# Transfers that build the sums of x, issued step by step, and output stores on another queue

## Chip, cores and metric

The kernel runs on one core of a Trainium2 chip. The metric is the time of one execution on the device in microseconds (us), as the median of several runs; less is better. The core has five engines with a queue of instructions each: TensorE (PE in the profile; its weight loads are PEld), VectorE (DVE), ScalarE (ACT), GpSimd (POOL) and SyncE (SP). An engine takes its queue in order and waits at an instruction until the data it needs is there. SP and POOL are used here to issue transfers (DMAs), which 16 DMA engines carry out. SP's transfers form one DMA queue, POOL's another.

## The reference

Four images x of 128 channels and 96 x 96 pixels go through two non-local blocks, one after the other. A block is attention over pixels: every one of the 9216 pixels is a query, and the 2304 pixels of a 2 x 2 max-pooled map are the keys and values.

```python
g_x     = maxpool2(conv1x1(x, g_w, g_b))        # values, 64 channels x 2304
theta_x = conv1x1(x, theta_w, theta_b)          # queries, 64 channels x 9216
phi_x   = maxpool2(conv1x1(x, phi_w, phi_b))    # keys, 64 channels x 2304
f    = jnp.einsum('bqc,bck->bqk', theta_x, phi_x)
attn = jax.nn.softmax(f, axis=-1)
y    = jnp.einsum('bqk,bkc->bqc', attn, g_x)
W_y  = conv1x1(y, W_w, W_b)                     # back to 128 channels
W_y  = W_y * inv + (bn_beta - bn_mean * inv)    # batch norm, inference form
return W_y + x
```

The output of the first block is the input of the second. Everything is float32.

## The kernel before

**Blocks, pairs, slots.** Four images times two layers make eight blocks, in the order of `ORDER`. An image stays in one SBUF tile `xt` [128, 9216], and a block adds its result into that tile. A block has nine *pairs* of 1024 queries. The keys are 18 tiles of 128, and a pair works through them in nine *slots* of two tiles: TensorE makes the scores of two tiles (L584), ScalarE their exponentials (L589), VectorE adds these up (L596, L598), and TensorE multiplies the exponentials of the slot before with the values (L606). There are 72 pairs, so 648 slots. Two pairs, an "even" and an "odd" one, make a *cycle* of 18 slots (`CYCLE`), numbered 0 to 17. One loop over `t` (L904) writes all slots out; whatever else is to be done hangs on a slot number of it. For TensorE, VectorE, ScalarE and SP this written order is the order of their queues (`manual_schedule`, L98 to L100). POOL isn't in that list: the framework's scheduler orders POOL's queue.

**The end of a pair.** When all values of a pair are summed, ScalarE copies the result out of PSUM into a tile `halves` (L613, `values`). There are two such tiles, so a pair takes the tile of the pair two before it. This copy is at slot 9 for the even pair and at slot 0 of the next cycle for the odd one. `turn` and `invert` make 1 / (sum of exponentials) on VectorE (L656 to L674). `invert` stands at slot 13 for the even pair and at slot 6 of the next cycle for the odd one. It ends with eight transfers on SP's queue: four that write the inverses as rows into a corner of the tile `stage` (L680) and four that spread each row over 64 partitions of `halves` (L685). `normalise` (L695) multiplies by them, at slots 1 and 10 of the next cycle. `multiply` (L701) projects back to 128 channels at slots 3 and 13 of the next cycle, and `add` follows at once: ScalarE adds the shift (L712), and POOL issues a transfer that adds `halves` into `xt` (L716, "the x add"). In the second layer POOL then issues the store of these pixels to the output (L726). The last two pairs do without the adding transfer.

**Units: keys and values of the next block.** While a block runs, the keys and values of the next one are made in six *units* of 16 image rows, two units in 18 slots. A unit makes its products with fewer multiplications, by use of sums of parts of x: `sums[0]` ("one"), `sums[1]` ("two"), each with a low half (partitions 0 to 63) and a high half, and `half`, a copy of half of `two[high]` in the low partitions. These tiles exist once and are used by all units in turn. A unit has four stages on TensorE, at the slots of `UNITS`: 15, 16, 18, 20 for units 0, 2, 4 of a block and 25, 26, 28, 30 for units 1, 3, 5, counted from the start of the cycle and 18 more for each further two units. The first stage reads x alone. The second reads `two[high]` (L460) and then, at the end of its slot and ahead of the values, `half` (`second_rest`, L463, seen as L441 `unit_ps<-stage`, since `half` lies in `stage`). The third reads `one`, the fourth `two[low]`.

**Building the sums.** `build` and `build_rest` (L412 to L430) issue the transfers. SP loads `one` (L416) and `two[high]` (L417) out of `xt`. POOL adds into `one[high]` and `one[low]` (L422, twice, `sums<-x`) and adds `one[high]` into `two[high]` (L422, `sums<-sums`, "the high add"). SP then copies `half` (L423), loads `two[low]` (L429), and POOL adds `two[high]` into it (L430). For unit 0 all this is written at slot 9 of the block's first cycle (`BUILD`). For the others `build` is written at the slot of the third stage of the unit before it, and `build_rest` at that of the fourth.

Of the kernel before, what the change touches and what calls it, by code (L numbers as in the profile page):

```python
# [12 lines left out]
ALU = mybir.AluOpType  # L13
# [3 lines left out]
P = 128  # L17
B, C, CI, H, W = 4, 128, 64, 96, 96
# [14 lines left out]
PT = 2 * QT  # L33
# [6 lines left out]
UN = 4 * W  # L40
# [1 line left out]
UB = 2 * UK // 32  # L42
TB = NKT // 2
UNITS = ((15, 16, 18, 20), (25, 26, 28, 30))
BUILD = 9
AFTER = ((1, 1, 2, 4, 5), (1, 2, 2, 3, 4))
THETAS = (6, 5)

# [6 lines left out]
CYCLE = 2 * NB  # L55
# [6 lines left out]
def shifted_blocks(ctx: ExitStack, tc: tile.TileContext, x: bass.AP, layers, out: bass.AP, flag):  # L62
# [24 lines left out]
    nc = tc.nc  # L87
# [26 lines left out]
    sums = [const.tile([P, 2, UN], F32, name=f"sums_{i}") for i in range(2)]  # L114
# [4 lines left out]
    def load_x(b, n=6):  # L119
        xt = xp.tile([C, HW], F32, tag="x", name=f"x_{b}")  # L120
        src = x[b].rearrange("c h w -> c (h w)")
        for i in range(n):
            nc.sync.dma_start(out=xt[:, ts(i, HW // n)], in_=src[:, ts(i, HW // n)])
        return xt
# [274 lines left out]
    class Unit:  # L399
# [12 lines left out]
        def build(self):  # L412

            low, high = slice(0, CI), slice(CI, P)
            one, two = sums
            nc.sync.dma_start(out=one, in_=self.pixels(0, slice(0, P)))  # L416
            nc.sync.dma_start(out=two[high], in_=self.pixels(1, low))  # L417
            for dst, src in (
                (one[high], self.pixels(0, low)), (two[high], one[high]),
                (one[low], self.pixels(1, low)),  # L420
            ):
                nc.gpsimd.dma_start(out=dst, in_=src, accum_op=ALU.add)  # L422
            nc.sync.dma_start(out=self.half, in_=two[high, :, UN // 2 :])  # L423

        def build_rest(self):

            low, high = slice(0, CI), slice(CI, P)
            two = sums[1]
            nc.sync.dma_start(out=two[low], in_=self.pixels(1, high))  # L429
            nc.gpsimd.dma_start(out=two[low], in_=two[high], accum_op=ALU.add)  # L430

        def both(self, *some):
            for c in range(2):
# [25 lines left out]
        def second(self):  # L459
            self.part(self.blk.w.mixed[CI:, 0, :], sums[1][CI:, :, : UN // 2], 0)  # L460
# [80 lines left out]
    class Pair:  # L541
# [164 lines left out]
        def add(self):  # L706

            cols = ts(self.p, PT)
            here = self.blk.xt[:, cols]
            if self.number < late:  # L710
                for h in range(2):
                    nc.scalar.activation(  # L712
                        self.halves[:, ts(h, QT)], self.pss[h], AF.Identity,
                        bias=self.blk.w.shift,
                    )
                nc.gpsimd.dma_start(out=here, in_=self.halves, accum_op=ALU.add)  # L716
                engine = nc.gpsimd
            else:
                for h in range(2):
                    dst = here[:, ts(h, QT)]  # L720
                    nc.vector.scalar_tensor_tensor(
                        dst, self.pss[h], self.blk.w.shift, dst, op0=ALU.add, op1=ALU.add
                    )
                engine = nc.sync
            if self.blk.store is not None:
                engine.dma_start(out=self.blk.store[:, cols], in_=here)  # L726

        def finish(self, check, result):

# [34 lines left out]
    def thetas(both):  # L764
        pss = two_banks(f"theta_ps_{both[0].name}")

        def part(i, rows, c):
            pair = both[i]
            return (
                pss[i][ts(c, CI), :], pair.blk.w.theta[rows, :],  # L770
                pair.blk.xt[rows, ts(2 * pair.p + c, QT)],
            )

        def take():
            for i in range(2):
                both[i].take_theta(pss[i])

        return crosswise(part, take)
# [20 lines left out]
    def begin(n):  # L799

        blocks[n].xt = xs[ORDER[n][0]]
        blocks[n].begin_keys()
# [66 lines left out]
    def later(t, step):  # L869
        tails.setdefault(t, []).append(step)  # L870

    for n in range(1, len(blocks)):
        cycle = (n - 1) * NP * NB // CYCLE * CYCLE
        for u in range(NU):
            unit = Unit(blocks[n], u)
            at = [cycle + u // 2 * 2 * CYCLE // 2 + i for i in UNITS[u % 2]]
            for i, t in enumerate(at):
                assert t not in stages
                stages[t] = (unit, i)
            if u == 0:  # L880
                later(cycle + BUILD, lambda n=n: begin(n))
                later(cycle + BUILD, unit.build)
                later(cycle + BUILD, unit.build_rest)
            else:
                later(free[0], unit.build)
                later(free[1], unit.build_rest)
            free = at[2:]
            when = [at[3] + i for i in AFTER[u % 2]]
            later(when[0], lambda unit=unit: unit.pool(1))
            if u == 0:  # L890
                later(when[0], unit.centring)
            later(when[1], lambda unit=unit: unit.pool(0))
            later(when[2], unit.spread)
            for i in range(2):
                later(when[3 + i], lambda unit=unit, i=i: unit.square(i))
# [8 lines left out]
    for t in range(total + 1):  # L904
        q, s = 2 * (t // CYCLE), t % CYCLE
        even, odd = pairs[q : q + 2] if t < total else (None, None)
        first, second, take = None, *pending
        pending = (None, None)
        unit, stage_of = stages.get(t, (None, None))
        assert unit is None or (t not in keys and second is None)  # L910
        if t in keys:
            n, i = keys[t]
            first, *pending = blocks[n].chunks(i)
        elif unit:
            first = (unit.first, unit.second, unit.third, unit.fourth)[stage_of]
            second = unit.second_rest if stage_of == 1 else None
            take = (unit.first_sum, unit.second_sum, unit.third_sum, unit.fourth_sum)[stage_of]
        elif t < total and s == THETAS[q > 0]:
            if q < late:
                first, *pending = thetas(pairs[q + 1 : q + 3])  # L920
            else:
                first, take = odd.theta_alone()
        elif t == total - 1:
            second, take = even.multiply, even.add
        elif gone and s in PROJECT:
            pair = gone[PROJECT.index(s)]
            second, take = pair.multiply, pair.add
        if t < total:
            now, j = divmod(t, NB)
            if s == 0 and q:  # L930
                gone = pairs[q - 2 : q]
            if t in loads:
                xs[loads[t]] = load_x(loads[t])
        for i in range(KB):
            if t < total:
                pairs[now].scores(j * KB + i, rowwise=stage_of == 1 and i == 1)
            if i == 0 and first:
                first()
        if second:
            second()  # L940
        for i in range(KB):
            if t < total:
                pairs[now].add_up(j * KB + i)
            if i == (stage_of == 1) and take:
                take()
        if t == 0:
            b0.batch(FIRST - 1)
        if t - 1 in keys and t < NB:
            b0.batch(keys[t - 1][1])
        if t:  # L950
            before, j = divmod(t - 1, NB)
            for k in ends.get(t, range(j * KB, (j + 1) * KB)):
                pairs[before].values(k)
        if t < total:
            for i, pair in enumerate(gone):
                if s == NORM[i]:
                    pair.normalise()
            for i, pair in enumerate((even, gone[1] if gone else None)):
                if pair is None:
                    continue  # L960
                if s in (TURNS[i], TURNS[i] + 1):
                    pair.turn(s - TURNS[i])
                sooner = q == late and i == 0
                if s == (TURNS[0] + 2 if sooner else HALVES[i]):
                    pair.add_halves()
                if s == (TURNS[0] + 2 if sooner else INVERT[i]):
                    pair.invert()
            if q == late and s == 15:
                even.normalise()
        if t == total - 1:  # L970
            odd.last_denominators()
        for i, k in squares.get(t, []):
            b0.square(i, k)
        for step in tails.pop(t, []):
            step()
        for step in after.pop(t, []):
            step()
# [323 lines left out]
```

## Time and profile before

| | us |
|---|---|
| median of 3 runs | 2540.0 |
| lowest, highest | 2537.94, 2541.27 |
| the profiled execution, its own time | 2539.5 |
| its span, first to last instruction | 2537.7 |

The mean granted clock of TensorE in the profiled execution is 0.995 of full speed. Some groups of instructions and transfers that the change touches or that stand near it:

| line | engine | what | times | mean or median |
|---|---|---|---|---|
| L613 | ACT | copy of `halves` out of PSUM | 71 | 1012 ns |
| L716 | POOL | issue of the x add, 512 KB | 70 | 5.3 us to landing |
| L726 | POOL | issue of a store, 512 KB | 34 | 3.2 us to landing |
| L422 | POOL | adds from x, 192 KB | 84 | 4.7 us to landing |
| L422, L430 | POOL | adds from a sum, 192 KB | 84 | 4.0 us to landing |
| L416 | SP | load of `one`, 384 KB | 42 | |
| L417, L429 | SP | loads of `two`, 192 KB | 84 | |
| L423 | SP | copy of `half`, 96 KB | 42 | |
| L680 | SP | rows of inverses, 1 KB | 284 | |
| L685 | SP | rows spread over 64 partitions, 64 KB | 284 | |

How to read what is shown further on. In the list of waits a line says which engine and line waited for which, then the total in us, the number of times and the longest. A timeline line gives the start in us from the span's start, the length in us, the engine (with q: its queue's own work, such as the issue of a transfer), line, operation, the tiles written and read, shapes and number, and in brackets the idle time before it with what ended it. For a transfer the length is that of its issue, not of its movement; when it has landed shows in whoever waits for it. A table by stretches gives the stretch, its length, then the busy time and number of instructions of each engine, the granted clock, the busy share of the DMA engines and GB/s.

### The profile page before, as it was taken

What the parts mean: (1) busy time and instruction counts of PE and PEld (TensorE: products, weight loads), DVE (VectorE), ACT (ScalarE), POOL (GpSimd) and SP (SyncE); (2) the same over time, 40 slices, a digit from 0 to 9 for tenths busy, and PEclk for the clock granted to TensorE, in tenths of its full rate; (3) what the DMA queues carried; (4) which work ended last, traced back from release to release, by engine and by line L of the source; (5) the groups of instructions that cost most, each with busy time, mean ns of one, the idle gap of its engine ahead of it and who ended that gap; (6) DMA issues with size and microseconds to landing.
All of it is one profiled execution on the core that took longest, in us unless ns stands there. A gap on an engine that the chain in (4) does not pass through costs nothing.

```text
span 2537.7 us, 56492 instructions
## 1 busy us (share of the span) xinstructions
PE 2487.6 (98%) x23391; PEld 945.2 (37%) x23391; DVE 2190.6 (86%) x2947; ACT 1671.8 (66%) x1836; POOL 233.9 (9%) x278
## 2 busy tenths in 40 slices
PE   9998999999999999998999999999999999999998
PEld 5344453433333333333333333333333333333333
DVE  7997988998879997997887999799987899878777
ACT  5665666666666666665666666666666666666664
POOL 0011001100011101110001110111000111000000
PEclk9999999999999999999999999999999999999999
DMA  5356444553356535555335663555434555333333
GB/s 181 42 78 131 41 51 65 73 62 26 26 84 87 85 45 82 75 69 125 26 26 83 87 87 43 82 75 72 55 23 38 77 86 94 43 43 42 40 38 52
DMA packets 96981, 167.62 MB, mean 66 GB/s; under 512 B 17346, under 2 KB 74060, under 8 KB 96716
## 3 DMA queue, kind: packets, MB, share of 16 engines
q1 hardware_dynamic: 62756, 76.29, 26.9%
q0 software_dynamic: 33792, 87.57, 20.3%
q8 instruction: 185, 3.03, 0.5%
q14 instruction: 80, 0.66, 0.1%
q10 hardware_dynamic: 168, 0.07, 0.0%
HBM read 19.21 MB, written 18.87 MB: 15 GB/s over the span
## 4 chain that ended last, share of the span: by engine, by line
PE 73%; DMA 16%; DVE 6%; issue 2%; ACT 2%; SPq 2%; POOL 0%; DVEq 0%; POOLq 0%; ACTq 0%
PE av L606 33%; PE sc L584 33%; DMA x<-halves 8%; DMA sums<-x 4%; DVE sum L598 3%; PE unit_ps L435 2%; PE theta_ps L268 2%; PE W_ps L701 2%; DMA sums<-sums 1%; ACT exp L589 1%; DMA halves<-stage 1%; SPq L680 1%; SPq L685 1%; ACT halves L613 1%; DMA stage<-both 0%
## 5 line engine op out<-in xcount | busy, mean ns | idle before, releaser
L589 ACT ACTIVATE exp<-sc,nshift 128x1024 f32<-128x1024 f32 x1296 | 1396.6, 1114 | 720.2 <-PE sc L584 708.0
L598 DVE TENSOR_TENSOR sum<-sum,exp 128x1024 f32<-128x1024 f32 x1151 | 1407.5, 1223 | 244.1 <-ACT exp L589 184.6
L584 PE MATMUL sc<-theta,phi 64*64 64x512 f32 x10368 | 1291.8, 590 | 3.1 <-ACT exp L589 3.0
L606 PE MATMUL av<-exp,gT 64*64 64x512 f32 x10368 | 1249.8, 592 | 29.4 <-ACT halves L613 29.3
L606 PEld LDWEIGHTS av<-exp,gT 64*64 64x64 f32 x10368 | 418.1, 133 | 715.1 <-issue 651.6
L584 PEld LDWEIGHTS sc<-theta,phi 64*64 64x64 f32 x10368 | 424.2, 133 | 680.0 <-issue 589.5
L422 POOL DMA_DIRECT2D sums<-x x84 | 82.4, 1160 | 836.9 <-DMA sums<-x 535.2
L716 POOL DMA_DIRECT2D x<-halves x70 | 70.8, 1011 | 836.9 <-ACT halves L712 836.8
L613 ACT COPY halves<-av 128x1024 f32<-128x1024 f32 x71 | 71.9, 1012 | 75.1 <-DMA x<-halves 49.8
L596 DVE TENSOR_TENSOR sum<-exp,exp 128x1024 f32<-128x1024 f32 x72 | 88.0, 1222 | 30.3 <-ACT exp L589 30.2
L657 DVE TENSOR_REDUCE parts<-turned 128x16 f32<-128x512 f32 x142 | 97.4, 686 | 4.9
L656 DVE STREAM_TRANSPOSE turned<-sum 128x512 f32<-128x512 f32 x142 | 100.1, 705 | 0.5
L712 ACT ACTIVATE halves<-W_ps,shift 128x512 f32<-128x512 f32 x140 | 88.8, 694 | 0.8 <-PE W_ps L701 0.8
L701 PE MATMUL W_ps<-halves,WT 64*64 64x512 f32 x568 | 75.2, 590 | 3.8 <-DVE halves L695 3.6
L495 DVE TENSOR_REDUCE stage<-stage 128x192 f32<-128x768 f32 x84 | 77.8, 940 | 0.0
L536 DVE STREAM_TRANSPOSE gT<-stage 32x192 f32<-32x192 f32 (+1 forms) x224 | 71.5, 319 | 3.8
L268 PE MATMUL theta_ps<-x,thetaT 64*64 64x512 f32 x560 | 74.0, 589 | 0.0
L695 DVE TENSOR_TENSOR halves<-halves 128x512 f32<-128x512 f32 x71 | 48.7, 685 | 26.7 <-DMA halves<-stage 26.7
L435 PE MATMUL unit_ps<-sums,mixed 64*64 64x384 f32 x504 | 70.2, 484 | 0.0
L430 POOL DMA_DIRECT2D sums<-sums x42 | 33.8, 805 | 303.9 <-DMA stage<-both 131.4
L669 DVE STREAM_TRANSPOSE four<-parts 32x32 f32<-32x32 f32 x284 | 56.4, 198 | 2.9
L692 DVE TENSOR_TENSOR halves<-halves 128x512 f32<-128x512 f32 x71 | 48.5, 683 | 0.0
(114 smaller groups left out, 753.9 us busy)
## 6 DMA issues: line engine op xcount, KB each, us to landing
x<-halves POOLq DMA_DIRECT2D x70, 512.0 KB, 5.3
halves<-stage SPq DMA_DIRECT2D x284, 64.0 KB
out_dram<-x POOLq DMA_DIRECT2D x34, 512.0 KB, 3.2
sums<-x SPq DMA_DIRECT2D x42, 384.0 KB
sums<-x SPq DMA_DIRECT2D x84, 192.0 KB
sums<-x POOLq DMA_DIRECT2D x84, 192.0 KB, 4.7
sums<-sums POOLq DMA_DIRECT2D x84, 192.0 KB, 4.0
x<-in_x_dram SPq DMA_DIRECT2D x18, 768.0 KB
```

The costliest lines, as they stand in the source:

```text
L268: nc.tensor.matmul(out, lhsT=lhsT, rhs=rhs, start=step == 0, stop=step == 1)
L435: nc.tensor.matmul(bank[ts(c, CI), :UN], lhsT=lhsT, rhs=rhs[:, c, :], start=True, stop=True)
L584: nc.tensor.matmul(ps[ts(c, CI), ts(h, QT)], lhsT=self.blk.keys_of(k, c, h), rhs=self.th[ts(h, CI), :], start=True, stop=True,)
L589: nc.scalar.activation(e, ps, AF.Exp, bias=nshift)
L596: nc.vector.tensor_add(self.sum, self.es[0], e)
L598: nc.vector.tensor_add(self.sum, self.sum, e)
L606: nc.tensor.matmul(self.av[ts(h, CI), ts(r, QT)], lhsT=self.blk.gT[ts(r, CI), k, :], rhs=e[ts(r, CI), ts(h, QT)], start=(k == 0), stop=(k ...
L613: nc.scalar.copy(self.halves, self.av)
L656: nc.vector.transpose(self.turned, self.sum[:, ts(h, QT)])
L657: nc.vector.tensor_reduce(self.parts[:, ts(h, QT // SQ)], self.turned.rearrange("p (b k) -> p b k", k=SQ), AX.X, ALU.add,)
L701: nc.tensor.matmul(self.pss[h][ts(c, CI), :], lhsT=self.blk.w.W[ts(h, CI), ts(c, CI)], rhs=self.y[ts(h, CI), :], start=True, stop=True,)
L712: nc.scalar.activation(self.halves[:, ts(h, QT)], self.pss[h], AF.Identity, bias=self.blk.w.shift,)
```

## The change

`BUILD` is replaced by `BUILDS`, a slot for each of six steps, the first list for units 0, 2, 4 and the second for units 1, 3, 5. `build` no longer issues anything; it returns six steps, which are written at these slots: load `one` and `two[high]`; the two adds into `one`; load `two[low]`; the high add; the copy of `half`; the add into `two[low]`. The copy of `half` now comes after the load of `two[low]`. The stores of the output leave `add` and become `put`, which is written three slots (`STORE`) after `add` and issues on SP; for the last pairs, which have no adding transfer, `put` is called at once, on SP as before.

```diff
-BUILD = 9
+BUILDS = ((10, 11, 12, 13, 14, 15), (18, 19, 20, 21, 23, 23))
+STORE = 3
...
             low, high = slice(0, CI), slice(CI, P)
             one, two = sums
-            nc.sync.dma_start(out=one, in_=self.pixels(0, slice(0, P)))
-            nc.sync.dma_start(out=two[high], in_=self.pixels(1, low))
-            for dst, src in (
-                (one[high], self.pixels(0, low)), (two[high], one[high]),
-                (one[low], self.pixels(1, low)),
-            ):
+
+            def add(dst, src):
                 nc.gpsimd.dma_start(out=dst, in_=src, accum_op=ALU.add)
-            nc.sync.dma_start(out=self.half, in_=two[high, :, UN // 2 :])
-
-        def build_rest(self):
-
-            low, high = slice(0, CI), slice(CI, P)
-            two = sums[1]
-            nc.sync.dma_start(out=two[low], in_=self.pixels(1, high))
-            nc.gpsimd.dma_start(out=two[low], in_=two[high], accum_op=ALU.add)
+
+            def load():
+                nc.sync.dma_start(out=one, in_=self.pixels(0, slice(0, P)))
+                nc.sync.dma_start(out=two[high], in_=self.pixels(1, low))
+
+            def load_rest():
+                nc.sync.dma_start(out=two[low], in_=self.pixels(1, high))
+
+            def add_one():
+                add(one[high], self.pixels(0, low))
+                add(one[low], self.pixels(1, low))
+
+            def copy_half():
+                nc.sync.dma_start(out=self.half, in_=two[high, :, UN // 2 :])
+
+            return (
+                load, add_one, load_rest, lambda: add(two[high], one[high]), copy_half,
+                lambda: add(two[low], two[high]),
+            )
...
                 nc.gpsimd.dma_start(out=here, in_=self.halves, accum_op=ALU.add)
-                engine = nc.gpsimd
             else:
...
-                engine = nc.sync
+                self.put()
+
+        def put(self):
             if self.blk.store is not None:
-                engine.dma_start(out=self.blk.store[:, cols], in_=here)
+                cols = ts(self.p, PT)
+                nc.sync.dma_start(out=self.blk.store[:, cols], in_=self.blk.xt[:, cols])
...
             if u == 0:
-                later(cycle + BUILD, lambda n=n: begin(n))
-                later(cycle + BUILD, unit.build)
-                later(cycle + BUILD, unit.build_rest)
-            else:
-                later(free[0], unit.build)
-                later(free[1], unit.build_rest)
-            free = at[2:]
+                later(cycle + BUILDS[0][0], lambda n=n: begin(n))
+            for i, step in zip(BUILDS[u % 2], unit.build()):
+                later(cycle + u // 2 * CYCLE + i, step)
...
             pair = gone[PROJECT.index(s)]
             second, take = pair.multiply, pair.add
+            later(t + STORE, pair.put)
```

Steps given to `later` are written at the end of their slot (L974), after the slot's `invert`.

## The prediction

> **What bounds the kernel now.** I read the page's busy times first, then the waits of all engines, then the timelines of one cycle in which a unit is built, and last the clock after long idles.
>
> ```profile
> PE 2487.6 (98%) x23391; PEld 945.2 (37%) x23391; DVE 2190.6 (86%) x2947; ACT 1671.8 (66%) x1836; POOL 233.9 (9%) x278
> ...
> PE av L606 <- ACT halves L613: 29.3, 14, 7.5
> PE unit_ps L441 <- DMA sums<-sums: 3.4, 1, 3.4
> ACT halves L613 <- DMA x<-halves: 49.8, 17, 9.2
> ```
>
> TensorE is busy 98% of the span, so it sets the end: a change gains at most what TensorE waits, and each wait added to TensorE is paid in full. Its named wait is 29.3 us in 14 places: values of the next pair (L606) wait until `halves` is copied out (L613), and that copy waits for the x add (L716) that still reads the buffer. L441's wait of 3.4 us, and 0.5 us more on its copy in the same list, belong to one unit that is fed late.
>
> After an idle of some us the clock is lower too. In each of these stretches TensorE has just resumed:
>
> ```profile
> core 0: us, PE busy (x) PEld busy (x) DVE busy (x) ACT busy (x) POOL busy (x), PEclk, DMA share, GB/s
> 231.70:237.30 5.60, 5.58 (x30) 3.66 (x34) 2.50 (x5) 0.67 (x1) 1.73 (x2) 0.50 0.55 69
> 731.70:735.70 4.00, 3.96 (x24) 1.35 (x28) 2.86 (x3) 2.01 (x2) 1.94 (x2) 0.57 0.20 33
> 1195.70:1199.90 4.20, 4.20 (x20) 1.25 (x24) 3.13 (x5) 1.94 (x2) 0.00 (x0) 0.51 0.00 0
> 1365.90:1370.60 4.70, 4.70 (x32) 1.65 (x36) 3.05 (x3) 2.38 (x3) 1.94 (x2) 0.64 0.33 52
> 1987.90:1991.80 3.90, 3.87 (x20) 1.28 (x24) 2.77 (x3) 2.00 (x2) 1.94 (x2) 0.56 0.22 36
> ```
>
> The column after the five busy times is the granted clock. Length times (1 - clock) is 2.8, 1.7, 2.1, 1.7 and 1.7 us: 10.0 us lost, 2.0 per idle. All that waiting costs now is therefore 29.3 + 3.9 + 10.0 = 43 us: the most that can come back.
>
> **The change, part by part.** The built programs have the same instructions in the same order on TensorE, VectorE and ScalarE. On POOL's queue the four adds of a unit still stand ahead of the x add, so the new slots do not separate those; only the 34 stores are gone from it. What differs is SP's queue, which holds loads, copy, rows (L680) and broadcasts (L685). Before, a unit gave it load, load, copy, rest of the load. Now the copy comes last, and for units 0, 2 and 4 of a block ("even" units: copy at slot 14, inverse at slot 13) it stands behind the four rows and four broadcasts of the inverse. For odd units the copy (slot 5) stays ahead of the inverse (slot 6). That is 7 x 3 = 21 even units. A queue knows no slots: a load goes when its turn comes and its buffer is read, so moving unit 0's load from slot 9 to 10 costs nothing.
>
> *The copy behind the broadcasts.* One even unit before, on SP, VectorE and TensorE:
>
> ```profile
> 1486.86 0.60 SPq L423 DMA_DIRECT2D stage<-sums  x1
> 1487.50 0.61 SPq L429 DMA_DIRECT2D sums<-x  x1
> 1489.12 2.79 SPq L680 DMA_DIRECT2D stage<-both  x4
> 1492.09 10.54 SPq L685 DMA_DIRECT2D halves<-stage  x4
> ...
> 1489.13 0.21 DVE L674 TENSOR_REDUCE notes<-both 32x2 f32<-32x64 f32 x1
> ...
> 1496.28 0.50 PE L441 MATMUL unit_ps<-stage,mixed 64*64 64x192 f32 x4
> ```
>
> VectorE ends the inverse at 1489.34; the broadcasts start 2.75 us later, and TensorE reads the copy 6.94 us after 1489.34. How long do broadcasts take to land? VectorE's L695 shows it where it waits for them:
>
> ```profile
> 2355.51 3.46 SPq L685 DMA_DIRECT2D halves<-stage  x4
> ...
> 2366.76 0.69 DVE L695 TENSOR_TENSOR halves<-halves 128x512 f32<-128x512 f32 x1 [1.07 <-DMA halves<-stage]
> ...
> 2504.36 3.80 SPq L685 DMA_DIRECT2D halves<-stage  x4
> ...
> 2518.38 0.69 DVE L695 TENSOR_TENSOR halves<-halves 128x512 f32<-128x512 f32 x1 [3.65 <-DMA halves<-stage]
> ```
>
> 11.25 us in the first, 14.02 us in the second, where POOL issued an x add at 2505.41 beside them. Does a transfer behind them on SP's queue wait for that? A load right behind shows it:
>
> ```profile
> 1603.27 3.51 SPq L685 DMA_DIRECT2D halves<-stage  x4
> 1606.87 2.32 SPq L416 DMA_DIRECT2D sums<-x  x1
> ...
> 1617.59 1.97 POOL L422 DMA_DIRECT2D sums<-x  x2 [24.68 <-DMA sums<-x]
> ```
>
> Landed 10.7 us after its issue and 14.3 us after the first broadcast; the same load issued at 1472.95, eight us behind broadcasts, was there 6.0 us later (add at 1478.97). So it waits. For the copy's own time behind them I take 1.0 us, an estimate between 0 (it lands with the last broadcast) and 2.34 (issue 229.38, used by L441 at 231.72 with a free queue).
>
> TensorE's new wait per even unit: 2.75 + 11.25 + 1.0 - 6.94 = 8.1 us, or 2.75 + 14.02 + 1.0 - 6.94 = 10.8 us with the x add beside. In the unit shown, POOL's last add (L430, 1490.74) waited for L429, stuck behind the copy, and the x add went at 1491.35. Now the rest of the load goes early, so that add can go when the one before has landed (1486.86) and the x add at about 1487.5, 4.6 us before the broadcasts; its median to land is 5.3 us, so they hardly meet. In unit 0 everything is later: x add 1350.72, so about 1346.9, beside broadcasts that would start at 1347.6. I take 8.1 us for 15 units and 10.8 for 6 (the first unit of all has no x add): 121 + 65 = 186 us. What else this makes late: the values queued behind L441 on TensorE, and through them exps and sums, which only follow.
>
> *Clock.* Each such idle is as long as the longest above, so 21 x 2.0 = 42 us more, with 1.7 to 2.8 as its ends.
>
> The Trainium skill, "TensorE: Matmul & The Clock Gate", Part 1, says that an idle window of about 3.4 us halves the clock and a busy one restores it. By the page a drop costs at least half of 3.4 us, an estimate of 36 us for 21 units instead of 42; the rows above agree with the halving and with its length.
>
> The skill's "DMA: Bandwidth & Descriptors", Queues, rings and completion order, speaks against my main term: it says that completion is not first-in-first-out per issuing engine. Taken to its end, the copy would wait only for its issue. But it also says that each ring is consumed in order, and the load that landed in 10.7 us instead of 6.0 agrees with that half; I go by the row. By the first half alone the sum would be that of the first rival below.
>
> *What comes back.* With TensorE some 10 us later at slot 16, the copy of `halves` at slot 0 finds its x add landed, and the late chains after the loads of x have the same slack: all 43 us are taken as returned, with 29 (the clock losses aside) as the low end.
>
> *Stores.* On POOL they leave; their waits there (222.5 us of an engine busy 9%) were hidden by TensorE, so 0; gain at most what is in the 43. On SP a store stands ahead of a unit's load. Its 512 KB took a median of 3.2 us to land, so the adds come up to 3.2 us later; cover is the 8.6 us between the high add's landing (1486.86) and its first use by TensorE (1495.43), so 0. If that cover were gone it would cost up to 3.2 us a unit, but inside the same wait. The store's wait for the x add holds the odd unit's load behind it; that add needs TensorE's slot 0 first anyway.
>
> Sum: 186 + 42 - 43 = +185 us on 2539.5 us of the profiled execution (span 2537.7) = 2724.5; the median lies 0.5 above, so 2725 us.
>
> Ends: 21 x (7.1 + 1.7) - 43 = +142 (copy lands with the last broadcast), and 21 x (10.8 + 1.3 + 2.8) - 29 = +284 (x add always beside, the copy's 2.34 in full): 2682 to 2824.
>
> **Rivals.** *The copy is held by its issue alone* (ends on the other side). If other rings let it pass, it is issued after the broadcasts' 3.46 us and lands 2.34 later: 2.75 + 3.46 + 2.34 - 6.94 = 1.6 us for 21 units, 34 us, no clock drop: 34 - 43 = -9, 2531 us. It decides below 43 / 21 = 2.05 us per unit. For it: SP issues all four broadcasts in 3.46 us. Against: the load's 10.7 us. 0.07.
>
> *No wait at all*: slack elsewhere hides the copy, and the 43 us come back: 2497 us. Against: 6.94 us of slack against 15. 0.02.
>
> *Light*: all broadcasts run alone and the clock stays up: 21 x 8.1 - 43 = +127, 2667 us. For: the x add goes earlier; against: five clock drops after shorter idles. 0.12.
>
> *Heavy*: the x add stays beside the broadcasts in every unit, since POOL's order is the same and the stores delay it: 21 x (10.8 + 2.8) - 43 = +243, 2783 us. For: before, it landed beside them in most such cycles. 0.15.
>
> **How the numbers follow.** Forecast 0.64, between 2690 and 2765 by itself. Range 2665 to 2800: it takes in light and heavy and leaves out the two rivals below (0.09) and some of the upper end. A difference of 0.2% is about what a measurement of this kernel can tell. Slower by more: 0.64 + 0.12 + 0.15 = 0.91; faster 0.08; within 0.2%: 0.01, taken from the issue-only rival, whose time is nearest to no change.
>
> **What would show it.** TensorE's L441 waits for the copy's transfer in 21 places, 8 to 11 us each, and granted clock near 0.5 for some 4 us after; L606's 29.3 us on L613 near zero; SP's copy issued behind four broadcasts in even units and ahead of them in odd ones. L441 waits under 2 us would prove the forecast wrong; so would waits at odd units.

## The result, and the profile after

| | median, us | lowest to highest | runs |
|---|---|---|---|
| before, beside the changed kernel | 2536.27 | 2530.12 to 2541.27 | 6 |
| changed kernel | 2745.55 | 2743.19 to 2750.59 | 6 |

The changed kernel takes 1.0827 times as long (95% interval 1.0808 to 1.0846). Its profiled execution spans 2743.2 us against 2537.7, so 205.5 us more.

Busy times of the changed kernel, each as total, share of the span and number of instructions:

```profile
PE 2527.4 (92%) x23391; PEld 1568.1 (57%) x23391; DVE 2195.4 (80%) x2947; ACT 1667.2 (61%) x1836; POOL 213.5 (8%) x244
```

The number of matmuls is the same, but TensorE now idles 2743.2 - 2527.4 = 215.8 us, against 50.1 before. It is also busy 39.8 us longer with the same work, which points to a lower clock. Where the idle time stands is told by the list of waits:

```profile
PE unit_ps L449 <- DMA stage<-sums: 189.1, 20, 11.3
...
ACT halves L621 <- PE av L614: 35.4, 71, 0.6
...
PE unit_ps L449 <- DMA sums<-sums: 10.5, 1, 10.5
```

L449 is L441 of before. It waits for the transfer `stage<-sums`, the copy of `half`, in 20 places. In one more place (the fifth unit made during block 1) it waits for the high add. Together that is 199.6 us, and 21 is the number of even units. The copy out of PSUM (L621, L613 before) now has only waits for TensorE in the list; its line with the x add, 49.8 us before, is gone.

One even unit (block 5, unit 4) shows how it comes about. The timelines of SP, VectorE, POOL and TensorE:

```profile
1608.14 0.59 SPq L426 DMA_DIRECT2D sums<-x  x1
1616.86 2.90 SPq L688 DMA_DIRECT2D stage<-both  x4
1619.87 6.07 SPq L693 DMA_DIRECT2D halves<-stage  x4
1626.00 2.49 SPq L433 DMA_DIRECT2D stage<-sums  x1
1628.54 2.48 SPq L736 DMA_DIRECT2D out_dram<-x  x1
```

```profile
1616.87 0.21 DVE L682 TENSOR_REDUCE notes<-both 32x2 f32<-32x64 f32 x1
```

```profile
1612.82 0.83 POOL L419 DMA_DIRECT2D sums<-sums  x1 [2.84 <-issue]
1617.18 0.81 POOL L419 DMA_DIRECT2D sums<-sums  x1 [3.53 <-PE sc L592]
1617.79 1.12 POOL L724 DMA_DIRECT2D x<-halves  x1
```

```profile
1623.16 1.09 PE L592 MATMUL sc<-theta,phi 64*64 64x512 f32 x8
1633.52 0.58 PE L449 MATMUL unit_ps<-stage,mixed 64*64 64x192 f32 x2 [9.27 <-DMA stage<-sums]
...
1634.18 3.65 PE L614 MATMUL av<-exp,gT 64*64 64x512 f32 x14
```

The source of the copy had long landed: POOL's next add, which needs the high add too, went at 1617.18. Yet the copy stands on SP behind four rows (L688) and four broadcasts (L693), goes at 1626.00, and is read at 1633.52. TensorE was done with its scores at 1624.25 and stands still for 9.27 us. The values (L614) wait behind L449 in its queue.

Two stretches after this wait: the first begins when TensorE resumes. Columns: stretch, length, busy time and number of each engine, granted clock, busy share of the DMA engines, GB/s.

```profile
core 0: us, PE busy (x) PEld busy (x) DVE busy (x) ACT busy (x) POOL busy (x), PEclk, DMA share, GB/s
1633.60:1638.10 4.50, 4.50 (x26) 3.03 (x30) 1.10 (x3) 0.00 (x0) 0.00 (x0) 0.50 0.02 10
1638.30:1642.30 4.00, 4.00 (x40) 2.62 (x36) 1.77 (x2) 2.12 (x2) 0.00 (x0) 0.94 0.00 0
```

For 4.5 us the clock is 0.50 and 26 matmuls get done; then 40 fit into a shorter stretch. Over all clock records of the trace, the time that TensorE was busy at the lower clock, times (1 - clock), is 47.2 us in 23 drops, against 10.4 us in 6 before; this sum is called the half clock's cost below. Of the 23 drops, 21 are at the even units and cost 45.5 us; two at the program's end cost 1.7 and nothing.

### The profile page after: what moved, and what is told of

Its sections match the earlier page's. It is cut to its first block, busy times and chain, and to the rows that moved or that the text cites. A ratio compares the mean times of both kernels' runs of the same rounds, so it can differ in the third digit from the quotient of the medians.

```text
span 2743.2 us, 56475 instructions
## 1 busy us (share of the span) xinstructions
PE 2527.4 (92%) x23391; PEld 1568.1 (57%) x23391; DVE 2195.4 (80%) x2947; ACT 1667.2 (61%) x1836; POOL 213.5 (8%) x244
## 4 chain that ended last, share of the span: by engine, by line
PE 68%; DVE 8%; DMA 7%; SPq 4%; issue 2%; ACT 2%; DVEq 0%; ACTq 0%
PE av L614 32%; PE sc L592 30%; DMA stage<-sums 5%; DVE sum L606 4%; SPq L693 4%; PE unit_ps L443 2%; PE theta_ps L269 2%; PE W_ps L709 2%; ACT exp L597 1%; DMA stage<-both 1%; DMA halves<-stage 1%; PE unit_ps L449 1%; DVE parts L665 1%; SPq L688 1%; DVE turned L664 1%
## 5 line engine op out<-in xcount | busy, mean ns | idle before, releaser
L592 PE MATMUL sc<-theta,phi 64*64 64x512 f32 x10368 | 1468.8, 593 | 3.0 <-ACT exp L597 2.9
L614 PE MATMUL av<-exp,gT 64*64 64x512 f32 x10368 | 1427.8, 604 | 0.0
L614 PEld LDWEIGHTS av<-exp,gT 64*64 64x64 f32 x10368 | 716.1, 136 | 411.2 <-issue 223.3
L592 PEld LDWEIGHTS sc<-theta,phi 64*64 64x64 f32 x10368 | 705.5, 134 | 410.5 <-issue 200.8
L449 PE MATMUL unit_ps<-stage,mixed 64*64 64x192 f32 x168 | 29.5, 433 | 189.1 <-DMA stage<-sums 189.1
L476 DVE TENSOR_TENSOR stage<-stage,unit_ps 128x192 f32<-128x192 f32 x84 | 27.5, 349 | 138.7 <-PE unit_ps L449 138.7
L449 PEld LDWEIGHTS unit_ps<-stage,mixed 64*64 64x64 f32 x168 | 12.6, 167 | 217.2 <-issue 212.7
L709 PE MATMUL W_ps<-halves,WT 64*64 64x512 f32 x568 | 91.9, 592 | 4.5 <-DVE halves L703 4.3
L621 ACT COPY halves<-av 128x1024 f32<-128x1024 f32 x71 | 71.9, 1013 | 35.4 <-PE av L614 35.4
L269 PE MATMUL theta_ps<-x,thetaT 64*64 64x512 f32 x560 | 88.8, 589 | 0.0
L419 POOL DMA_DIRECT2D sums<-sums x84 | 68.7, 817 | 256.8 <-PE W_ps L709 86.0
```

The source lines that it names most:

```text
L269: nc.tensor.matmul(out, lhsT=lhsT, rhs=rhs, start=step == 0, stop=step == 1)
L592: nc.tensor.matmul(ps[ts(c, CI), ts(h, QT)], lhsT=self.blk.keys_of(k, c, h), rhs=self.th[ts(h, CI), :], start=True, stop=True,)
L614: nc.tensor.matmul(self.av[ts(h, CI), ts(r, QT)], lhsT=self.blk.gT[ts(r, CI), k, :], rhs=e[ts(r, CI), ts(h, QT)], start=(k == 0), stop=(k ...
L709: nc.tensor.matmul(self.pss[h][ts(c, CI), :], lhsT=self.blk.w.W[ts(h, CI), ts(c, CI)], rhs=self.y[ts(h, CI), :], start=True, stop=True,)
```

## The experiments

The span of an experiment is compared with 2537.7 us of before or 2743.2 of the changed kernel; a ratio is against the kernel before in runs beside it.

**1. The copy ahead of the inverse.**

```diff
-BUILDS = ((10, 11, 12, 13, 14, 15), (18, 19, 20, 21, 23, 23))
+BUILDS = ((10, 11, 12, 12, 12, 15), (18, 19, 20, 21, 23, 23))
```

> The changed kernel with one thing moved back: for units 0, 2 and 4 the high add and the copy of half are written at slot 12, so that the copy stands ahead of the rows and broadcasts of the inverse on SP's queue; loads, adds and stores stay as changed. Theory (the copy waits behind the broadcasts): TensorE's 199.6 us of waits at L449 and the half clock after them go, so at least 235 us go and the time is 2500 to 2540 us; the load of two[low], still ahead of the copy, lets the x add go some 4 us earlier than in the kernel before, which should take part of the 29 us at the copy of halves away. Rival (the adds themselves, spread over slots, come too late, or the stores on SP hold them up): the waits at L449 stay and the time is about 2740 us.

2499.31 us, ratio 0.9871 (0.9854 to 0.9887). Busy times, waits, then SP's timeline in the cycle of one unit:

```profile
PE 2478.0 (99%) x23391; PEld 1061.3 (42%) x23391; DVE 2191.6 (88%) x2947; ACT 1669.2 (67%) x1836; POOL 213.8 (9%) x244
```

```profile
ACT halves L621 <- PE av L614: 35.4, 71, 0.6
...
PE unit_ps L449 <- DMA sums<-sums: 3.6, 1, 3.6
```

```profile
1455.20 0.59 SPq L433 DMA_DIRECT2D stage<-sums  x1
1455.89 2.80 SPq L688 DMA_DIRECT2D stage<-both  x4
1459.05 4.01 SPq L693 DMA_DIRECT2D halves<-stage  x4
```

With the copy ahead of the rows, all 20 waits are gone; the 3.6 us that remain are the 3.4 of before. Half clock costs 4.1 us. So the whole loss hangs on the place of one transfer, and the rest of the change, left as it is, makes the kernel faster. POOL's timeline in the same cycle shows why:

```profile
1451.35 0.83 POOL L419 DMA_DIRECT2D sums<-sums  x1 [2.78 <-issue]
1455.72 0.81 POOL L419 DMA_DIRECT2D sums<-sums  x1 [3.53 <-PE sc L592]
1456.32 1.12 POOL L724 DMA_DIRECT2D x<-halves  x1
```

The last add goes 4.4 us after the high add, for its load no longer waits behind the copy, and the x add follows. Over the even units the x add is issued 2.7 us ahead of the broadcasts (median); before, 0.2 us behind their start. It lands in time for the copy of `halves`, whose wait of 29.3 us on TensorE is gone.

**2. As 1, stores on POOL behind the x add, as before.**

```diff
                 nc.gpsimd.dma_start(out=here, in_=self.halves, accum_op=ALU.add)
+                if self.blk.store is not None:
+                    nc.gpsimd.dma_start(out=self.blk.store[:, cols], in_=here)
...
-            later(t + STORE, pair.put)
```

> As the run with the copy ahead of the inverse, but the 34 stores go back to POOL's queue, right after the x add, as in the kernel before. Theory (the stores cost nothing on either queue, TensorE covers them): within 0.3% of the run with the copy ahead. Rival (a store ahead of a unit's loads on SP delays the adds, up to 3.2 us a unit, until TensorE waits): this run is faster than the run with the stores on SP by 0.5% or more. Third (the stores' waits on POOL hold up the next unit's adds): it is slower by 0.5% or more.

2498.92 us, ratio 0.9869 (0.9852 to 0.9885): the same as 1 on the same chip. The stores cost nothing on either queue. Against the kernel before, this one has the same order on POOL, and on SP the load of `two[low]` stands ahead of the copy in all 42 units (the first unit's transfers also stand behind a few loads of weights at the start): that swap is the gain.

**3. As 1, with POOL's queue in the written order too.**

```diff
-               mybir.EngineType.SP}
+               mybir.EngineType.SP, mybir.EngineType.Pool}
```

> As the run with the copy ahead of the inverse, with POOL in the list of engines whose queue follows the written order, so that the x add stands between the adds of a unit and no longer behind the last of them. Theory (what is left of the waits at the copy of halves comes from the x add's place behind the adds): those waits go to near zero and the time falls by 3 to 15 us against the run with the copy ahead. Rival (the x add is late because of the loads of x or the broadcasts running beside it): the time stays within 0.2%.

2501.0 us, ratio 0.9877 (0.9861 to 0.9894). The x add now stands between the adds, and nothing is won. The waits that it could have removed were gone already.

**4. The kernel before, with the copy of even units behind the inverse.** Its queues differ from before by that alone.

```diff
-            nc.sync.dma_start(out=self.half, in_=two[high, :, UN // 2 :])
+            if self.u % 2:
+                self.copy_half()
...
+            if u % 2 == 0:
+                later(at[0] - 1, unit.copy_half)
```

> The kernel before with one part of the change alone: for units 0, 2 and 4 the copy of half is written one slot ahead of its reader, behind the inverse; loads, adds and stores stay as before. Theory (this place alone makes the loss): TensorE waits for the copy's transfer some 20 times, 8 to 12 us each, and the time is 2720 to 2760 us. Rival (it takes the spread adds or the stores on SP as well): 2530 to 2600 us.

2747.79 us, ratio 1.0845 (1.0827 to 1.0863). The waits (the line's number has moved by three):

```profile
PE unit_ps L446 <- DMA stage<-sums: 193.8, 20, 11.8
...
PE unit_ps L446 <- DMA sums<-sums: 10.6, 1, 10.6
```

Half clock costs 47.7 us. This place alone makes the loss of the change, in the same 21 units, and all else in the change is not needed for it.

**5. The copy stays where the change put it, but goes to ScalarE's DMA queue.** Is it the queue's order, or the DMA engines that all queues share?

```diff
-                nc.sync.dma_start(out=self.half, in_=two[high, :, UN // 2 :])
+                engine = nc.sync if self.u % 2 else nc.scalar
+                engine.dma_start(out=self.half, in_=two[high, :, UN // 2 :])
```

> The changed kernel, but for units 0, 2 and 4 ScalarE issues the copy of half, at the same slot 14, so that it is in another DMA queue than the broadcasts, which still run at that time. Theory (the copy waits its turn in SP's queue): it lands 2 to 4 us after its issue, the waits at L449 fall from 199.6 us to under 25 us, and the time is 2495 to 2520 us. Rival (the broadcasts keep the 16 DMA engines busy, whatever the queue): the copy still lands with the last broadcasts, and the time is over 2650 us.

2604.77 us, ratio 1.03 (1.0259 to 1.0342): between the two times that were expected. The waits for the copy:

```profile
PE unit_ps L450 <- DMA stage<-sums: 67.6, 15, 8.3
```

There are units with no wait and units with a long one. First one without, in the timelines of ScalarE's queue, POOL (the x add), SP and TensorE, then one with a wait:

```profile
723.79 0.60 ACTq L434 DMA_DIRECT2D stage<-sums  x1
...
724.52 1.04 POOL L725 DMA_DIRECT2D x<-halves  x1
...
724.94 9.73 SPq L694 DMA_DIRECT2D halves<-stage  x4
...
728.60 0.36 PE L450 MATMUL unit_ps<-stage,mixed 64*64 64x192 f32 x2
```

```profile
2091.65 0.60 ACTq L434 DMA_DIRECT2D stage<-sums  x1
...
2091.25 1.12 POOL L725 DMA_DIRECT2D x<-halves  x1
...
2091.98 10.81 SPq L694 DMA_DIRECT2D halves<-stage  x4
...
2104.44 0.58 PE L450 MATMUL unit_ps<-stage,mixed 64*64 64x192 f32 x2 [7.91 <-DMA stage<-sums]
```

Issued 1.15 us ahead of the first broadcast and 0.7 us ahead of the x add, the copy is read 4.8 us later, on time. Issued 0.33 us ahead of the broadcasts, and 0.4 us after an x add, it is read 12.8 us later. The lead over the broadcasts alone does not decide it: another copy went 1.17 us ahead of them, but 0.3 us after an x add, and was read 10.2 us later (2013.15 to 2023.32). So the other queue removes the order in SP's queue, and the waits for the copy fall from 189.1 to 67.6 us; but a copy that starts beside other transfers still gets through slowly. The Trainium skill, "DMA: Bandwidth & Descriptors", Issuing engines are not separate DMA queues, says that starting transfers from several engines saves only the time of the issue. The 12.8 us agree with it, and what was saved fits it too: the copy is issued 0.4 us ahead of the first broadcast (median of the even units) instead of 6.1 us behind it, and 121.5 us less of waits are 6.1 us for each of 20 units. But that is not the copy's own issue of 0.60 us. It is about the issue of the four broadcasts ahead of it on SP, 6.07 us in the unit shown with the result.

A price of its own: once the copy's issue held ScalarE for 14.2 us until the high add had landed, and the exponentials behind it made TensorE wait 13.1 us.

**6. The copy between the second and the third broadcast.** How much of the wait is made by the broadcasts that are issued ahead of it?

```diff
-        def invert(self):
+        def invert(self, between=None):
...
+                if i == 2 and between:
+                    between()
```

(`between` is the even unit's copy, and its high add moves to slot 12.)

> The changed kernel, but for units 0, 2 and 4 the copy of half stands in SP's queue behind the four rows and two of the four broadcasts, and ahead of the other two (the high add is written at slot 12 for it). Theory (the queue is worked off in order, so the copy waits for the bytes ahead of it): with half the broadcasts ahead the wait per unit falls by 5 to 6 us, from 9.5 to about 4 us, 65 to 100 us in all with about half of the clock loss, and the time is 2570 to 2640 us. Rival (the copy waits until all broadcasts are through, by contention or by a shared counter): 2700 us or more. Rival (only the place behind the last broadcast hurts): about 2500 us.

2689.13 us, ratio 1.0622 (1.0599 to 1.0644). Waits:

```profile
PE unit_ps L449 <- DMA stage<-sums: 134.8, 20, 8.5
```

With L449's 6.0 us for the high add, the wait falls from 199.6 to 140.8 us, 2.8 us for each unit, where I had expected 5 to 6. Without the unit that waits for the high add, the copy is read 12 to 15 us after the inverse instead of 14.7 to 17.8.

**7. TensorE kept busy during the wait.** The product that precedes L449's wait is repeated, with the same result, to see how much of the loss is the clock's.

```diff
-            self.part(self.blk.w.mixed[CI:, 0, :], sums[1][CI:, :, : UN // 2], 0)
+            for n in range(1 if self.u % 2 else WARMING):
+                self.part(self.blk.w.mixed[CI:, 0, :], sums[1][CI:, :, : UN // 2], 0)
```

> The changed kernel, but in units 0, 2 and 4 the second stage's products from two[high] are made 28 times over, just ahead of the product that waits for the copy; each makes the same values again. At some 0.3 us a time they fill 8 to 9 us in which TensorE would have stood idle. Theory (some 47 us of the loss are matmuls at half clock after the idle): the idle at L449 falls under 45 us, the granted clock stays at 1, and although TensorE has more to do the time falls by 35 to 50 us, to 2695 to 2710 us. Rival (the slow start after the wait comes from refilling the other engines' queues): no gain, 2740 us or more.

With `WARMING = 28`: 2726.16 us, ratio 1.0764 (1.0739 to 1.0789). Half clock costs 19.0 us instead of 47.2, and the span is 19.0 us shorter, where I had expected 35 to 50. Of the 19.0, 8.7 us lie in one unit, the one that waits for the high add: there the repetitions ran at half clock themselves (17.66 us from the first to the start of the last, against 8.95 in another unit).

**8. As 6, without the two broadcasts behind the copy.** In the cycles of even units two of the four rows of inverses are not spread, so half of a pair's queries are scaled with what stood there, and the output is not the reference's. Did those two, issued later, still hold the copy?

```diff
                 if i == 2 and between:
                     between()
+                    break
```

> As the run with the copy between the broadcasts, but the two broadcasts behind the copy are left out for the even pairs of units 0, 2 and 4, so a quarter of a pair's queries there is scaled with old values and the output is not the reference's. In the run with all four the copy was at TensorE 12 to 15 us after the inverse. Theory A (the rings of SP's queue run out of step and the later broadcasts compete with the earlier ones for the one partition they all read): without them the copy is there some 10 us after the inverse, L449 waits about 3 us a unit, and the time is 2540 to 2600 us. Theory B (two broadcasts simply take that long): the wait stays near 7 us a unit and the time is 2670 us or more.

2642.39 us, ratio 1.0435 (1.0414 to 1.0455). Waits:

```profile
PE unit_ps L449 <- DMA stage<-sums: 88.2, 20, 6.4
```

With L449's 6.1 us for the high add, the wait falls from 140.8 to 94.3 us: 2.2 us a unit were due to transfers issued behind the copy. But 94.3 / 21 = 4.5 us a unit stay, with only two broadcasts ahead, and the time lies between the two that were expected. What stays is twice what the later two broadcasts made. The units of this trace divide it, the one that waits for the high add left aside: where no x add went near, or went 3.5 us or more ahead of the broadcasts, the copy was read 7.1 us after the first of them (four units); where it went 0.7 to 1.0 us ahead, 10.2 to 10.6 us after (three units).

**9. As 7, with 32 repetitions, and none in the unit that waits for the high add.**

```diff
-            for n in range(1 if self.u % 2 else WARMING):
+            for n in range(1 if self.u % 2 or self.name == "1_0_4" else WARMING):
```

> As the run that repeats the second stage's products, with 32 repetitions instead of 28 to fill the wait wholly, and none in the one unit (block 1, unit 4) whose sums come late anyway, where the repetitions cost 8.7 us at half clock before. Theory (matmuls at half clock after the idle cost 47 us, of which 28 came back): the loss to half clock falls under 10 us and the time is 2695 to 2715 us, although the repetitions may end up to 1 us after the copy has landed. Rival (the idle itself is all that counts): 2726 us or more.

2712.81 us, ratio 1.071 (1.0688 to 1.0731). Busy times:

```profile
PE 2679.9 (99%) x25871; PEld 1746.5 (64%) x25871; DVE 2193.0 (81%) x2947; ACT 1669.4 (62%) x1836; POOL 213.5 (8%) x244
```

TensorE does 2480 matmuls more than in the changed kernel, and the span is 32.7 us shorter (2710.5). Half clock costs 4.2 us, 43.0 less; 10.3 of these do not show in the span. Most of that is repetitions that end after the copy has landed: it is read 0.5 us after its landing in the mean, 0.14 where TensorE waits for it. The clock is thus a real part of the loss and not a reading of the profile alone.

**10. As 1, with a load of the next image seven slots later.** It aims at the one wait left in 1.

```diff
-    loads = {4 * NB + 7: 2, 31 * NB + 6: 3}
+    loads = {4 * NB + 14: 2, 31 * NB + 6: 3}
```

> The run with the copy ahead of the inverse, with the six loads of the third image moved from slot 7 to slot 14 of its cycle, behind the loads and the copy of block 1's unit 4 on SP's queue. Theory (the one wait left at L449, 3.6 us, and the half clock after it come from those loads standing ahead of the unit's): both go, 4 to 7 us less than with the copy ahead, 2492 to 2496 us. Rival (the loads then hold up the next unit's loads and the x add): within 0.2% or slower.

2493.42 us, ratio 0.9844 (0.9828 to 0.9861). L449 waits for no transfer any more, and

```profile
PE 2476.9 (99%) x23391; PEld 1059.3 (42%) x23391; DVE 2191.5 (88%) x2947; ACT 1670.5 (67%) x1836; POOL 214.1 (9%) x244
```

leaves 16.4 us of idle in a span of 2493.3. It is the fastest of all: the change with the copy put ahead of the inverse, and the load of one image (six transfers) moved. The intervals of its ratio and of 1's overlap; that the move helps is read from the wait of 3.6 us that is gone.

## Why the prediction was right, point by point

| term of the sum | forecast, us | measured, us |
|---|---|---|
| wait of TensorE for the copy, 21 units | +186 | +199.6 |
| new clock loss | +42 | +47.2 |
| what comes back | -43 | -43.6 (29.3 + 3.9 + 10.4) |
| sum | +185 | +203.2 of 205.5 |

**Where it waits.** 21 even units and no odd one, as forecast. Experiment 1 removes the wait by the copy's place, experiment 4 makes it by that place alone; so the cause is shown from both sides.

**How long: the term that was mis-sized.** For the unit shown the working goes: broadcasts 2.79 us after the inverse (forecast 2.75), copy read 13.65 us after the first of them (forecast 11.25 + 1.0 = 12.25), TensorE ready 7.17 us after the inverse (forecast 6.94); 2.79 + 13.65 - 7.17 = 9.27 us. The middle term is off. I had put 15 of the 21 units at 8.1 us, because the x add would go 4.6 us ahead of the broadcasts "so they hardly meet". It went 2.1 us ahead (median), and with its 4.7 us to landing it met them after all. I had worked this out in one unit of before, where the high add was issued 9.1 us ahead of the broadcasts; the median of the even units with an x add beside is 8.5 before, and 7.1 in the changed kernel. Three units were later still (two units 0 and a unit 2): with the x add 0.3 to 0.7 us ahead, the copy's issue came 9.0 to 10.6 us after the first broadcast, against 6.1 in the unit shown. So the 20 waits for the copy have a mean of 9.5 us, between the 8.1 and the 10.8 that I had for the two cases, and the twenty-first was 10.5. The 6 units 0 for which I had 65 us waited 62.8; the other 15, for which I had 121, waited 136.8.

That the x add makes the difference shows in the units of the changed kernel. The first unit of all has no x add beside it (SP and TensorE below); then come SP, POOL and TensorE in a unit where the x add went 0.66 us ahead of the broadcasts:

```profile
81.27 3.48 SPq L693 DMA_DIRECT2D halves<-stage  x4
...
93.19 0.58 PE L449 MATMUL unit_ps<-stage,mixed 64*64 64x192 f32 x2 [9.16 <-DMA stage<-sums]
```

```profile
1454.05 10.54 SPq L693 DMA_DIRECT2D halves<-stage  x4
...
1453.39 1.03 POOL L724 DMA_DIRECT2D x<-halves  x1
...
1469.00 0.59 PE L449 MATMUL unit_ps<-stage,mixed 64*64 64x192 f32 x2 [11.34 <-DMA stage<-sums]
```

The copy is read 11.9 us after the first broadcast in the one and 15.0 in the other. In the other units that wait for the copy it is 11.8 and 11.9 us with the x add 4.0 and 4.2 us ahead, 12.6 to 13.7 with 2.1 to 2.8, 13.8 to 14.5 with 1.2 to 1.9, and 14.7 and 15.1 with 0.3 and 0.6. So the two cases, 12.25 and 15.02, were sized nearly right; what was wrong is that most units lie between them. No run took the x add away in the other units.

**Clock.** 2.0 us per idle forecast; 47.2 us in 23 drops is 2.05, and 45.5 us at the 21 units 2.17. The low and high ends, 1.7 and 2.8, were not needed. Experiment 9 takes 43 of them back in the trace and 33 in the span.

**What comes back.** The wait on the copy of `halves` is gone as forecast. But the reason that I gave, more time through the lateness of TensorE, is not needed: experiment 1 loses that wait too with no lateness, by the earlier x add. I had seen that the x add would be earlier, and used it for the broadcasts alone.

**Stores.** Forecast at 0 on either queue; experiment 2, in the version without the wait, agrees with 0 (2498.92 against 2499.31).

**POOL.** The new slots didn't separate the four adds of a unit from the x add, as forecast, and by experiment 3 it would have changed nothing in the version without the wait.

**Rivals.** *The copy is held by its issue alone*: refuted on SP's queue by the 7.5 us between its issue (1626.00) and its use, where it had 2.34; the broadcasts' issue ahead of it was longer too, 6.07 us against 3.46. Experiment 5 shows what a queue without broadcasts gives. Yet the mechanism is no plain queue either: by experiment 8, transfers issued behind the copy held it for 2.2 us a unit. A single measured load had stood for "it lands behind them"; that gave the right size. *No wait at all*: refuted; its 2497 us are what experiment 1 reached (2499), by taking the wait away. *Light* (2667): no; the clock fell and the broadcasts did not run alone. *Heavy* (2783): no, though the time lies toward it, since the x add did land beside the broadcasts in part.

**What stays open.** How the DMA engines share their time between a copy, broadcasts and an adding transfer: experiments 5, 6 and 8 give the sums, not the order of packets.

## What to carry to other kernels

Slots only order an engine's queue: before a small transfer that TensorE needs soon is moved by a slot, list what stands between its old and its new place in that queue, and how long that takes to land; here 96 KB behind four broadcasts cost 8%. A swap in that list can also be worth something: with the copy still ahead of the broadcasts, the load of `two[low]` ahead of the copy made the kernel 1.3% faster. Work out a slack over all units, or in the median one, and not in the one that happens to be on the screen.

## What was not expected of the hardware

The clock's price hardly depends here on the length of the idle: the 21 drops at units cost 45.5 us with waits of some 9.5 us, and 42.3 us in experiment 8 with waits of some 4.5.

A transfer was held by others issued after it (2.2 us a unit, experiments 6 and 8). On another queue, a copy of 96 KB that started 0.4 us after an x add and 0.33 us ahead of broadcasts was read 12.8 us later, one that started ahead of both 4.8 us later (experiment 5).

Matmuls whose result is not needed can shorten a span: 2480 more of them, 32.7 us less (experiment 9).
